# Score products of 64 keys instead of 128: eight small tiles of the array instead of four, in attention and in some steps of a windowed linear attention

## The chip, the cores and the metric

The kernel runs on one core of one Trainium2 chip. The metric is the device time of the whole kernel in microseconds (us), the median of several runs. Smaller is better.

## What is computed

The input is one image of 256 channels and 64 x 64 pixels in float32. Two layers follow one another, and all arithmetic that matters here is float32.

```python
# layer 0: x + L0(group_norm(x)), 8 heads of 32 channels
q, k = sigmoid(Wq x), sigmoid(Wk x);  v = Wv x, normalised per head
for w in (1, 2, 4):                       # windows of 64/w pixels around each pixel
    wk, wkv = box sums of k and of k v^T over the window
    attn = (q . wkv) / (q . wk + 1e-6)
out = Wout concat(attn)
# layer 1 on t = 4096 tokens of 256 channels
dots = einsum('bhid,bhjd->bhij', q, k) * 256 ** -0.5
attn = softmax(dots);  t = t + (attn v) w_out
t = t + mixture of 8 experts, the best 2 per token
```

The change touches two places in which q of some pixels is multiplied with k of others: the windowed sums of layer 0, which the kernel computes as masked scores (q . k for each pixel pair, zeroed outside the window, then times v), and the softmax attention of layer 1.

## The kernel before, in words

The image's 4096 pixels are cut into 8 strips of 8 columns (512 tokens, one "chunk"); each strip has 8 bands of 8 rows, and a strip's part of two such 64-pixel cells is a tile of 128 tokens, 32 in all. Heads have 32 channels, so 4 heads fill the 128 partitions, and both layers go over 2 groups of 4 heads.

**Layer 0** runs from 0 to about 1035 us, one head group after the other. `prepare` makes q, k, v and running sums. `attend` then goes over the three windows. For each it does band steps first (two of the windows: loop over b, scores at line 609, values at line 640), and then strip steps (loop over ix, scores at line 678, values at line 694). A *job* is one tile of 128 keys against a run of query cells of one strip; `packed` puts as many jobs into one *step* as fit into 512 score columns, so a step holds one or two jobs in the strip loop. The step's 4 score banks (one per head, a pool of 6) are masked by `masked` (line 558, on VectorE, or on ScalarE and GpSimd for a head or two), and the values of line 694 are issued one step later, since `behind` puts them into a list that `tick` empties in the middle of the next step. Steps with one job are those of 384 or of 512 query columns: 56 for each head group, 112 in all.

The band steps at line 609 already take 64 keys at a time: for each of 4 heads two products, whose results go to partitions 0 to 63 and 64 to 127 of the head's bank. The strip steps at line 678 take 128 keys at a time.

**Layer 1's attention** runs from 1147 to 2307 us. It is 16 *blocks*: 8 query chunks of 512 by 2 head groups; each block has 32 steps, one for every key tile i. A step is:

```python
for hd in range(4):                          # line 991: 4 products, 128 keys x 512 queries
    sc[hd // 2][:, hd % 2, :] = k[hd, tile i] . q[hd, chunk]
pe[pair] = exp(sc / 16)                      # line 1001, ScalarE, twice 128 x 1024
total[pair] += pe[pair]                      # line 1008, VectorE, twice (not for i = 0 and 31)
# one step later, by tick():
acc[32 hd : 32 hd + 32] += v[i, hd] . pe[hd] # line 959: 4 products, 32 rows of output each
```

The order on TensorE is therefore scores of step i+1, values of step i, scores of i+2, and so on. Scores go to `two_banks` buffers of two banks each; there are 3 of them and a step takes 2. `pe` has 4 buffers, `acc` one. At a block's end come two more groups at line 959 (sums by a matrix of ones), a copy by ScalarE, and, some steps into the next block, a reciprocal (line 1056) and a multiplication (line 1032) on VectorE. In every other block from the fourth on, four steps also carry a projection (`project`, line 940) with an addition and statistics on VectorE.

In both places a product of 32 rows (channels) and 128 columns (keys) uses one row group of the array, and the four heads use its four row groups.

Of the kernel before, what the change touches and what calls it, by code (L numbers as in the profile page):

```python
# [30 lines left out]
P = 128  # L31
# [4 lines left out]
CH = 512  # L36
# [5 lines left out]
CELL = SW * SW  # L42
# [69 lines left out]
def tile_conv_attn_hybrid(ctx: ExitStack, tc: tile.TileContext, a: dict, out: bass.AP):  # L112
    nc = tc.nc
# [26 lines left out]
    def tok(i):  # L140
        return slice(P * i, P * (i + 1))

    def chunk(i):
        return slice(CH * i, CH * (i + 1))
# [18 lines left out]
    def behind(*stages):  # L163

        chains.append(list(stages))
# [20 lines left out]
    with ExitStack() as phase:  # L186
# [23 lines left out]
        with (  # L210
# [23 lines left out]
            for i in range(4):  # L234
                for k in range(KC):
                    at = slice(i * N // 4, (i + 1) * N // 4)
# [45 lines left out]
        rows = big.tile([P, NB, C // D, 4 * IMG], F32, tag="qk", name="rows")  # L282
# [255 lines left out]
        def step_done():  # L538
            tick()
            if chores:  # L540
                chores.pop(0)[1]()
# [3 lines left out]
        def masked(work, scs, used, pieces):  # L545


            turns[0] += 1
            sms = []
            for h, sc in enumerate(scs):  # L550
                sm = work.tile([P, CH], F32, tag="sm", name="sm", bufs=12)
                src, engine = sc, nc.vector
                if h == 1 or h == 3 and turns[0] % 2:
                    nc.scalar.copy(sm[:, :used], sc[:, :used])  # L554
                    src, engine = sm, nc.gpsimd
                for at, n, mk in pieces:
                    to, of = (z[:, at : at + n].rearrange("p (m n) -> p m n", n=mk.shape[-1]) for z in (sm, src))
                    engine.tensor_mul(to, of, mk.unsqueeze(1).to_broadcast(list(to.shape)))  # L558
                sms.append(sm)
            return sms  # L560

        def joined(pieces):

            out = []
            for at, n, mk, key in pieces:
                if out and out[-1][3] == key:
                    out[-1][1] += n
                else:
                    out.append([at, n, mk, key])
            return [piece[:3] for piece in out]  # L570

        def packed(jobs):

            steps = []
            for job in jobs:
                if not steps or sum(j[0] for j in steps[-1]) + job[0] > CH:
                    steps.append([])
                steps[-1].append(job)
            return steps

        def attend(g, work, ps, qk, v, ssum, rec, woT):
            bank = lambda: ps.tile([P, CH], F32, tag="acc", name="ps_acc", bufs=2)
            score = lambda: ps.tile([P, CH], F32, tag="sc", name="ps_sc", bufs=6)
            qT, kT = qk[:, 0], qk[:, 1]
            hs = [slice(D * h, D * (h + 1)) for h in range(4)]
            qcells = qT.rearrange("p (i n) -> p i n", n=CH)
            raw = big.tile([P, NCH, CH], F32, tag="raw", name="raw")
            for w in (2, 1, 0):
# [4 lines left out]
                for b in (1, 2, 0, 3) if r > 1 else ():  # L593
# [8 lines left out]
                    for step in steps:  # L602
                        scs = [score() for _ in range(4)]
                        at, places = 0, []
                        for n, i, lo, hi, kind in step:
                            for h in range(4):
                                for u in range(2):
# [5 lines left out]
                                        start=True,  # L613
                                        stop=True,
                                        skip_group_check=True,
# [44 lines left out]
                for ix in range(NCH):  # L660
                    acc = bank()
                    jobs = []
                    for jx, kind in ((ix - r, 1), (ix, 0), (ix + r, 2)):
                        if 0 <= jx < NCH and (kind or r == 1):
                            for m in (0, 3, 1, 2):
                                c0, c1 = max(0, 2 * m - r), min(SW, 2 * m + 2 + r)
                                key = kind, c0 - 2 * m + r, c1 - 2 * m + r
                                mk = mask[:, kind - 1, _MCELL0[w] :] if kind else mask0
                                mk = mk[:, key[1] : key[2]].rearrange("p n c -> p (n c)")
                                jobs.append((CELL * (c1 - c0), NB * jx + m, c0, c1, mk, key))  # L670
                    begun = [False]
                    steps = packed(jobs)
                    for step in steps:
                        scs = [score() for _ in range(4)]
                        at, places = 0, []
                        for n, i, c0, c1, *mk in step:
                            for h in range(4):
                                nc.tensor.matmul(  # L678
                                    scs[h][:, at : at + n],
                                    kT[hs[h], tok(i)],  # L680
                                    qT[hs[h], CH * ix + CELL * c0 : CH * ix + CELL * c1],
                                    start=True,
                                    stop=True,
                                    skip_group_check=True,
                                )
                            places.append((at, n, i, c0, c1, *mk))
                            at += n
                        sms = masked(work, scs, at, joined((p[0], p[1], *p[-2:]) for p in places))
                        step_done()

                        def use(places=places, sms=sms, acc=acc, begun=begun, ix=ix, last=step is steps[-1], raw=raw, r=r):
                            for at, n, i, c0, c1, *_ in places:
                                for h in range(4):
                                    nc.tensor.matmul(  # L694
                                        acc[hs[h], CELL * c0 : CELL * c1],
                                        v[:, i, hs[h]],
                                        sms[h][:, at : at + n],
                                        start=not begun[0],
                                        stop=last and at == places[-1][0],
                                        skip_group_check=True,  # L700
                                    )
                                begun[0] = True
                            if last and r > 1:
                                nc.vector.tensor_add(raw[:, ix, :], acc, raw[:, ix, :])
                            elif last:
                                nc.scalar.copy(raw[:, ix, :], acc)

                        behind(lambda: None, use)
# [35 lines left out]
        for g in range(KC):  # L744
            with tc.tile_pool(name="c_prep", bufs=1) as prep, psum("c_ps1", 2) as ps:
                of = prepare(g, prep, ps)
            with tc.tile_pool(name="c_work", bufs=1) as work, psum("c_ps2", 1) as ps:
                attend(g, work, ps, *of)
# [33 lines left out]
    with ExitStack() as phase:  # L782
# [9 lines left out]
        qk = big.tile([P, 2, KC, N], F32, name="qk")  # L792
# [5 lines left out]
        with (  # L798
# [23 lines left out]
            for n, by in enumerate((lambda k: ones[:, :1], lambda k: bqk[:, 4 + k : 5 + k])):  # L822
                for k in range(KC):
# [4 lines left out]
                        start=k == 0,  # L828
                        stop=k == KC - 1,
# [11 lines left out]
            for k in range(KC):  # L841
                for j in range(KC):
# [4 lines left out]
                        start=j == 0,  # L847
                        stop=j == KC - 1,
# [11 lines left out]
            for c in range(NCH):  # L860
# [29 lines left out]
                for i in range(NB * c, NB * (c + 1)):  # L890
                    pv = ps.tile([P, CH], F32, tag="mm", name="ps_mm")
                    for k in range(KC):
# [4 lines left out]
                            start=k == 0,  # L897
                            stop=k == KC - 1,
# [47 lines left out]
        with tc.If(tame > 0) as branch:  # L946
            with (
# [5 lines left out]
                def two_banks():  # L953
                    return ps.tile([P, 2, CH], F32, tag="two", name="ps_two", bufs=3)
# [26 lines left out]
                for qc in range(NCH):  # L981
                    for g in range(KC):
# [4 lines left out]
                        for i in range(NT):  # L987
                            sc = [two_banks() for _ in range(2)]
                            for hd in range(4):
                                hs = slice(D * hd, D * (hd + 1))  # L990
                                nc.tensor.matmul(  # L991
                                    sc[hd // 2][:, hd % 2, :],
                                    qk[hs, 1, g, tok(i)],
                                    qk[hs, 0, g, chunk(qc)],
                                    start=True,
                                    stop=True,
                                )
                            pe = work.tile([P, 4, CH], F32, name="pe", bufs=4)
                            pairs = [slice(0, 2), slice(2, 4)]
                            for pair, s in zip(pairs, sc):  # L1000
# [84 lines left out]
        with branch.Else():  # L1085


            with (
# [8 lines left out]
                for hd in range(2 * 4):  # L1097
                    g, hs = hd // 4, slice(D * (hd % 4), D * (hd % 4 + 1))
                    nc.vector.tensor_copy(ka[:D, :], qk[hs, 1, g, :])
                    for qc in range(NCH):  # L1100
                        qa = bigb.tile([D + 1, CH], F32, name="qa")
                        nc.vector.tensor_copy(qa[:D, :], qk[hs, 0, g, chunk(qc)])
                        for i in range(CH // P):
                            for c in range(NCH):
                                sc = ps.tile([P, CH], F32, tag="sc", name="ps_sc")
# [11 lines left out]
                        for i in range(NT):  # L1117
                            sc = ps.tile([P, CH], F32, tag="sc", name="ps_sc")
# [3 lines left out]
                            for j, lhsT in enumerate((v[:, i, D * hd : D * (hd + 1)], ones)):  # L1122
# [4 lines left out]
                                    start=i == 0,  # L1127
                                    stop=i == NT - 1,
                                    skip_group_check=True,
# [10 lines left out]
    with ExitStack() as phase:  # L1140
# [14 lines left out]
        def each(name):  # L1155
            return small.tile([P, NT, NE], F32, name=name)
# [33 lines left out]
        with ExitStack() as routing:  # L1190
# [7 lines left out]
            at = 0  # L1198
# [118 lines left out]
            for n in range(2):  # L1317
                at = each(f"at{n}")
# [12 lines left out]
                for i8 in range(0, NT, G):  # L1331
# [7 lines left out]
                    for i in range(G):  # L1339
# [4 lines left out]
                            start=n == 0 and i8 + i == 0,  # L1344
                            stop=n == 1 and i8 + i == NT - 1,
# [98 lines left out]
        with ExitStack() as ending:  # L1444
# [6 lines left out]
            for b in range(NB):  # L1451
                for i4 in range(0, NCH, 4):
# [4 lines left out]
                    for i in range(4):  # L1457
                        at = NB * (i4 + i) + b
# [43 lines left out]
```

## Time and profile before

| what | us |
|---|---|
| median of 3 runs (lowest, highest) | 2935.82 (2933.38, 2937.23) |
| the profiled execution | 2937.02 |
| its span, first to last instruction | 2935.2 |
| TensorE busy in the span | 2794.7 (95%) |
| VectorE busy | 2083.2 (71%) |
| ScalarE busy | 1533.0 (52%) |
| GpSimd busy | 720.3 (25%) |
| scores of attention, line 991 (4096 MATMULs) | 629.1 |
| values of attention, line 959 (4096 MATMULs) | 546.4 |
| strip scores of layer 0, line 678 (2688 MATMULs) | 245.3 |
| band scores of layer 0, line 609, 64 keys at a time (2560 MATMULs) | 104.9 in its forms |

How to read it: PE is TensorE's products, PEld its weight loads (the load of k or v into the array), DVE VectorE, ACT ScalarE, POOL GpSimd. A row gives line, engine, operation, result and operands, then the shape: "32\*128 32x512" is a product of 32 rows and 128 columns of the array with 512 columns of moving data. Each float32 product appears as two MATMULs and two weight loads, here called its two passes. Products that run beside one another overlap in the records, so their busy time is that of the group, and their ends are modelled while their starts are recorded: durations of groups are best taken from start to start. "Idle before" is the time in which the engine had nothing running ahead of an instruction, with what ended it.

### The profile page before, as it was taken

To read this page: it belongs to the slowest core of one execution; us is meant where nothing else is said; L and a number is where in the kernel's file an instruction comes from. 1 tells how busy PE (TensorE), PEld (TensorE's weight loads), DVE (VectorE), ACT (ScalarE), POOL (GpSimd) and SP (SyncE) were. 2 spreads that over 40 slices of the span, in tenths; PEclk is the share of its full clock that TensorE was granted. 3 is DMA by queue.
4 is the path that set the end of the run, shared out by engine and by line. 5 is a ranking of instruction groups with operands and counts; after the bars stand their busy time and mean duration, and the time that the engine had idled before them with its cause. 6 is when DMAs were issued, how large, how long until landed. Compare 5 with 4: busy or idle time off the path is not lost. (4 is left out here: it accounts for less than half of the span.)

```text
span 2935.2 us, 63107 instructions
## 1 busy us (share of the span) xinstructions
PE 2794.7 (95%) x26358; PEld 1352.3 (46%) x26358; DVE 2083.2 (71%) x3005; ACT 1533.0 (52%) x2134; POOL 720.3 (25%) x816
## 2 busy tenths in 40 slices
PE   6899999989999989999999999999999699999996
PEld 5466442735644354222222222222222268888884
DVE  5776768577677877999999999999999821111113
ACT  3242323124233213888888888888888622222222
POOL 1085858119485621000000000000000022222220
PEclk9999999999999999999999999999999879999997
DMA  5000000000000000000000000000000155555555
GB/s 142 6 3 3 2 3 2 7 1 3 4 2 3 1 19 1 5 5 5 5 5 5 5 5 5 5 5 5 5 5 5 53 182 200 191 189 195 192 196 198
DMA packets 97930, 137.35 MB, mean 47 GB/s; under 512 B 18242, under 2 KB 79272, under 8 KB 97636
## 3 DMA queue, kind: packets, MB, share of 16 engines
q1 hardware_dynamic: 82360, 105.31, 10.9%
q0 software_dynamic: 6912, 18.88, 2.2%
q10 hardware_dynamic: 8364, 9.02, 0.9%
q8 instruction: 210, 3.44, 0.5%
q14 instruction: 84, 0.69, 0.1%
HBM read 115.07 MB, written 18.12 MB: 45 GB/s over the span
## 5 line engine op out<-in xcount | busy, mean ns | idle before, releaser
L1001 ACT ACTIVATE pe<-ps_two 128x1024 f32<-128x1024 f32 x1024 | 993.1, 1022 | 150.0 <-PE ps_two L991 145.4
L1008 DVE TENSOR_TENSOR total<-total,pe 128x1024 f32<-128x1024 f32 x928 | 1058.2, 1217 | 0.0
L991 PE MATMUL ps_two<-qk 32*128 32x512 f32 x4096 | 629.1, 639 | 3.6 <-POOLq L946 1.9
L959 PE MATMUL ps_acc<-pe,v 128*32 128x512 f32 x4096 | 546.4, 605 | 0.1
L554 ACT COPY sm<-ps_sc 128x384 f32<-128x384 f32 (+4 forms) x486 | 232.4, 512 | 459.5 <-PE ps_sc L678 276.4
L558 POOL TENSOR_TENSOR sm<-sm,mask 128x192 f32<-128x192 f32 (+3 forms) x460 | 380.2, 861 | 231.6 <-ACT sm L554 231.0
L991 PEld LDWEIGHTS ps_two<-qk 32*128 32x128 f32 x4096 | 204.8, 183 | 418.7 <-PE ps_two L991 222.2
L558 DVE TENSOR_TENSOR sm<-ps_sc,mask 128x384 f32<-128x384 f32 (+3 forms) x708 | 324.2, 518 | 91.7 <-PE ps_sc L678 90.2
L1417 ACT ACTIVATE hid<-ps_hp,cols 128x256 f32<-128x256 f32 x288 | 136.4, 473 | 382.8 <-PE ps_hp L1416 382.0
L1266 POOL MEMSET on<- 128x256 f32 x1 | 0.3, 311 | 1175.1 <-PE ps_den L959 1175.1
L959 PEld LDWEIGHTS ps_acc<-pe,v 128*32 128x32 f32 x4096 | 80.7, 108 | 389.4 <-issue 376.2
L1416 PE MATMUL ps_hp<-xe,w 128*128 128x256 f32 x1152 | 257.0, 381 | 0.0
L1423 PE MATMUL ps_yp<-w,hid 128*128 128x256 f32 x1152 | 254.6, 379 | 0.0
L678 PE MATMUL ps_sc<-qk 32*128 32x192 f32 (+3 forms) x2688 | 245.3, 446 | 5.2 <-DVE sm L558 2.9
L1423 PEld LDWEIGHTS ps_yp<-w,hid 128*128 128x128 f32 x1152 | 216.4, 190 | 28.1
L1416 PEld LDWEIGHTS ps_hp<-xe,w 128*128 128x128 f32 x1152 | 208.5, 190 | 42.1 <-ACT hid L1417 5.0
L694 PE MATMUL ps_acc<-sm,v 128*32 128x192 f32 (+3 forms) x2688 | 216.6, 423 | 0.8 <-POOL sm L558 0.8
L1395 DVE TENSOR_SCALAR xe<-ps_tp,cols 128x256 f32<-128x256 f32 x72 | 35.9, 540 | 248.8 <-PE ps_tp L1391 228.7
L558 POOL TENSOR_TENSOR sm<-sm,ycut 128x384 f32<-128x384 f32 (+4 forms) x150 | 150.7, 1025 | 140.4 <-ACT sm L554 140.2
L678 PEld LDWEIGHTS ps_sc<-qk 32*128 32x128 f32 x2688 | 126.4, 186 | 124.0 <-DVE sm L558 70.4
L1425 DVE TENSOR_TENSOR y<-ps_yp,b 128x256 f32<-128x256 f32 x72 | 30.6, 425 | 208.1 <-PE ps_yp L1423 208.1
L558 DVE TENSOR_TENSOR sm<-ps_sc,ycut 128x512 f32<-128x512 f32 (+4 forms) x250 | 127.7, 562 | 64.8 <-PE ps_sc L609 62.7
(231 smaller groups left out, 2252.5 us busy)
## 6 DMA issues: line engine op xcount, KB each, us to landing
w<-in_L_ffn_W SPq DMA_DIRECT2D x72, 1024.0 KB
b<-in_L_ffn_b SPq DMA_DIRECT2D x36, 128.0 KB
rows<-in_x SPq DMA_DIRECT2D x16, 256.0 KB
zrows<-z SPq DMA_DIRECT2D x4, 1024.0 KB
y<-yrows SPq DMA_DIRECT2D x8, 512.0 KB
y<-yrows ACTq DMA_DIRECT2D x8, 512.0 KB
rec<-recs SPq DMA_DIRECT2D x60, 64.0 KB
x<-in_x ACTq DMA_DIRECT2D x4, 512.0 KB
```

Of the source, the lines that this page charges most:

```text
L554: nc.scalar.copy(sm[:, :used], sc[:, :used])
L558: engine.tensor_mul(to, of, mk.unsqueeze(1).to_broadcast(list(to.shape)))
L678: nc.tensor.matmul(scs[h][:, at : at + n], kT[hs[h], tok(i)], qT[hs[h], CH * ix + CELL * c0 : CH * ix + CELL * c1], start=True, stop=True, ...
L694: nc.tensor.matmul(acc[hs[h], CELL * c0 : CELL * c1], v[:, i, hs[h]], sms[h][:, at : at + n], start=not begun[0], stop=last and at == plac ...
L959: nc.tensor.matmul(to[D * hd : D * (hd + 1), :], lhsT(hd), rhs[:, hd, :], start=start, stop=stop, skip_group_check=True,)
L991: nc.tensor.matmul(sc[hd // 2][:, hd % 2, :], qk[hs, 1, g, tok(i)], qk[hs, 0, g, chunk(qc)], start=True, stop=True,)
L1001: nc.scalar.activation(pe[:, pair, :], s, AF.Exp, scale=C**-0.5)
L1008: add = nc.vector.tensor_add(to, first[:, pair, :] if i == 1 else to, pe[:, pair, :])
L1395: nc.vector.tensor_scalar(xe[:, k, :], tp[:, k, :], cols[:, gain], cols[:, shift], op0=ALU.mult, op1=ALU.add,)
L1416: nc.tensor.matmul(hp, w1[:, k, tok(n)], x_now[:, k, :], start=k == 0, stop=k == KC - 1)
L1417: nc.scalar.activation(hid[:, n, :], hp, AF.Gelu, bias=cols[:, n : n + 1])
L1423: nc.tensor.matmul(yp, hid[:, n, tok(j)], w2[:, n, :], start=n == 0, stop=n == NH - 1)
```

## The change

Where a strip step has one job, and in every attention step, each product of 128 keys becomes two of 64 keys: keys 0 to 63 of the tile give partitions 0 to 63 of the bank, and keys 64 to 127 give partitions 64 to 127. The moving data (512, or 384, query columns) are the same for both halves. A step issues eight products of 32 rows by 64 columns where it issued four of 32 by 128. Strip steps with two jobs keep products of 128 keys. What is computed, the buffers and the work of the other engines are as before.

```diff
@@ strip steps of layer 0
                         for n, i, c0, c1, *mk in step:
+                            rows = CELL if len(step) == 1 else P
                             for h in range(4):
-                                nc.tensor.matmul(
-                                    scs[h][:, at : at + n],
-                                    kT[hs[h], tok(i)],
-                                    qT[hs[h], CH * ix + CELL * c0 : CH * ix + CELL * c1],
-                                    start=True,
-                                    stop=True,
-                                    skip_group_check=True,
-                                )
+                                for u in range(0, P, rows):
+                                    nc.tensor.matmul(
+                                        scs[h][u : u + rows, at : at + n],
+                                        kT[hs[h], P * i + u : P * i + u + rows],
+                                        qT[hs[h], CH * ix + CELL * c0 : CH * ix + CELL * c1],
+                                        start=True,
+                                        stop=True,
+                                        skip_group_check=True,
+                                    )
@@ attention
                             for hd in range(4):
                                 hs = slice(D * hd, D * (hd + 1))
-                                nc.tensor.matmul(
-                                    sc[hd // 2][:, hd % 2, :],
-                                    qk[hs, 1, g, tok(i)],
-                                    qk[hs, 0, g, chunk(qc)],
-                                    start=True,
-                                    stop=True,
-                                )
+                                for u in range(2):
+                                    nc.tensor.matmul(
+                                        sc[hd // 2][CELL * u : CELL * (u + 1), hd % 2, :],
+                                        qk[hs, 1, g, P * i + CELL * u : P * i + CELL * (u + 1)],
+                                        qk[hs, 0, g, chunk(qc)],
+                                        start=True,
+                                        stop=True,
+                                        skip_group_check=True,
+                                    )
```

## The prediction

> **What bounds the kernel now.** I first took busy time by stage. Attention (lines 983 to 1008 and 959) runs from 1147 to 2307 us; the four other stretches hold all single-block steps of line 678. The columns are the stretch, its length, then busy time of PE, PEld, DVE, ACT and POOL with the number of instructions.
>
> ```profile
> 1147.40:2307.00 1159.60, 1157.80 (x8532) 311.98 (x8536) 1122.94 (x1070) 1008.19 (x1054) 0.00 (x0) 1.00 0.02 5
> 1726.50:1797.30 70.80, 70.80 (x530) 18.42 (x528) 68.90 (x63) 63.07 (x66) 0.00 (x0) 1.00 0.02 5
> 303.70:369.00 65.30, 65.30 (x789) 27.45 (x792) 52.64 (x125) 26.12 (x55) 59.20 (x72) 1.00 0.01 2
> 446.00:506.00 60.00, 60.00 (x544) 15.88 (x538) 49.08 (x89) 25.08 (x50) 52.95 (x50) 1.00 0.01 2
> ```
>
> PE is never out of work in any of them. In one attention block (second line: 32 key tiles for one query chunk and one head group, 70.8 us) DVE is free for only 1.9 us and ACT for 7.7. So PE sets the pace, and DVE is close behind. Busy is not the same as fast, so next the order of time of two steps. The first five rows are PE's, the last two ACT's, from the same stretch.
>
> ```profile
> 1700.61 1.31 PE L991 MATMUL ps_two<-qk 32*128 32x512 f32 x8
> 1701.85 1.07 PE L959 MATMUL ps_acc<-pe,v 128*32 128x512 f32 x8
> 1702.85 1.17 PE L991 MATMUL ps_two<-qk 32*128 32x512 f32 x8
> 1703.94 1.06 PE L959 MATMUL ps_acc<-pe,v 128*32 128x512 f32 x8
> 1704.94 0.70 PE L991 MATMUL ps_two<-qk 32*128 32x512 f32 x2
> ...
> 1701.81 1.94 ACT L1001 ACTIVATE pe<-ps_two 128x1024 f32<-128x1024 f32 x2 [0.15 <-PE ps_two L991]
> 1704.02 1.94 ACT L1001 ACTIVATE pe<-ps_two 128x1024 f32<-128x1024 f32 x2 [0.27 <-PE ps_two L991]
> ```
>
> A float32 product is two MATMULs (a group of 4 is x8). Starts of scores to starts of values take 1.24 us, then 1.10 us: every other group is held up. By its single records heads 0 and 1 start at 1700.609, heads 2 and 3 only at 1700.791, when an exponential (ended 1700.739) has given their score banks back (3 buffers, 2 needed a step). The loop over two steps: heads 0 and 1 of step i start, +1.20 their exponential starts, +1.02 it ends, +0.05 heads 2 and 3 of step i+1 start, +1.06 values start, +1.00 the scores of i+2 start: 4.33 us, 2.166 a step. PE alone would need 1.07 + 1.00 = 2.07.
>
> The form after the change exists already, in the band steps of line 609 (8 products of 32 rows by 64 columns). Same number of query columns, both forms:
>
> ```profile
> 956.94 0.93 PE L678 MATMUL ps_sc<-qk 32*128 32x384 f32 x8
> 957.80 1.06 PE L694 MATMUL ps_acc<-sm,v 128*32 128x512 f32 x8
> ...
> 888.07 0.90 PE L609 MATMUL ps_sc<-qk 32*64 32x384 f32 x16
> 888.90 0.98 PE L640 MATMUL ps_acc<-sm,v 64*32 64x448 f32 x16
> ...
> L678 PEld LDWEIGHTS ps_sc<-qk x2688: 181/184/333, 142.6 to 1005.5; 32*128 32x128 f32 x192
> ...
> L609 PEld LDWEIGHTS ps_sc<-qk x2560: 127/131/132, 232.3 to 946.9; 32*64 32x64 f32 x197
> ```
>
> Start to next group's start: 0.86 us with 128 keys a product, 0.83 with 64 (by the records 857 and 830 ns). A weight load is 181 against 127 ns.
>
> **What the Trainium skill says.** "TensorEngine Tiling (Array Packing)", Available Configurations and Key Properties: 32-row tiles come as four of 128 columns or eight of 64, the tiles work independently, and a change of mode drains the array. The trace agrees and prices the drain: from the last MATMUL's start, less the columns at 1.2 a ns, to the next group's start it is 90 to 96 ns in the 993 changes between lines 991 and 959, and 90 to 97 around line 609; there is a drain before and after. "TensorE: Matmul & The Clock Gate", LDWEIGHTS (loading the stationary operand): a load takes its columns over 1.2 ns, whatever the rows: 107 for 128, 53 for 64. The difference in the trace is 54. The same page, Part 3, gives about 4 ns from tile to tile; the records here show 6.7.
>
> **The change, part by part.** *One score group, nothing waiting.* By the records at 384 columns: first pass to second pass 427 ns before (107 load + 384/1.2), 373 in the 64-key form (53 + 320). The second pass of the last product starts 3 x 6.7 = 20 ns after the first one's before, 7 x 6.7 = 47 after. From there to the next group 410 in both. Sum: -54 + 27 = -27, which is 857 to 830. At 512 columns: 107 + 427 + 20 + 427 + 90 = 1071 (shortest measured group: 1070), after it 53 + 427 + 47 + 427 + 90 = 1044. Line 609 has no group of 512, but 256, 320, 384 and 448 columns give 617, 724, 830 and 937, a straight line that reaches 1044 there. I take -26.5.
>
> *Attention steps in the rhythm above.* Two links of the loop contain a load. Exponential after scores: -54 on the load, and the second pass of heads 0 and 1 ends with the 4th product instead of the 2nd, +13: -40. Heads 2 and 3 to values: -54, and the last product starts 3 x 6.7 after their first instead of 6.7, +13: -40. So -80 per two steps, -40 a step: 2.166 becomes 2.126. PE alone would then need 2.04, so the loop still holds.
>
> *How many steps.* The 510 score groups with a record take 1158 ns on average, 1070 unheld: 510 x 0.088 = 45 us of holding up. Two steps in rhythm hold up 1242 + 1098 - 2 x 1071 = 198 ns, so 45/0.198 x 2 = some 450 steps are in rhythm and 62 (block ends, steps with a projection of line 940) are not. 450 x 40 = 18.0 us, 62 x 26.5 = 1.6 us: **-19.6 us**.
>
> *Is DVE in the way?* Its additions start every 1.135 us, so 2.27 a step in 30 of 32 steps. It falls behind and catches up at the block's end. Block 1726.5: 70.8 - 1.3 = 69.5 us against 68.9 of work: 0.6 us stay free. The second test is the probability buffers (4): the exponential of step i+4 needs the addition of step i. The margin falls from 5.1 us at a block's start to 1.3 at its end (records of all blocks: 1.28 to 2.3); PE being 32 x 0.040 = 1.3 earlier there uses it up just so. I cost this at nothing; if the cover is 0.2 us short in each block, 16 x 0.2 = 3 us come back. ACT has 2 x 1.02 of work in a step of 2.126 and covers.
>
> *Single-block steps of layer 0.* The groups at line 678 of 384 (x640) and 512 columns (x256) are 896/8 = 112 steps. PE is busy throughout the stretches above, POOL for 59.2 of 65.3 and 53.0 of 60.0. 112 x 26.5 = **-3.0 us**; where the second pair waits for a bank as in attention, up to 112 x 40 = 4.5. Lower bound zero, if POOL's masks end last.
>
> *Added.* (512 + 112) x 4 = 2496 more products, 4992 MATMULs and as many loads. No wait is added: the built program has the same semaphore waits before heads 0 and 1 and before heads 2 and 3, and the order on DVE, ACT, POOL and SP is unchanged; no DMA is moved. Queued behind PE's wait are, as before, the values of line 959. Supply of instructions: over the 5120 MATMULs of lines 609 and 640, PE idles 1.8 + 1.6 + 1.1 us under "issue", 0.9 ns each; at worst 4992 x 0.9 = 4.4 us. I take zero, since attention issues 24 MATMULs in 2.1 us where line 609's steps issue 32 in 1.7.
>
> *Sum*: 19.6 + 3.0 = 22.6 us. The profiled execution took 2937.0 us, a span of 2935.2 and 1.8 around it: 2914.4. The median of the runs shown is 1.2 below it: 2935.8 - 22.6 = **2913.2**.
>
> **The rivals.**
> *A, the loop keeps its length and only the drain-to-drain time shrinks.* If exponential and bank release don't move, a step gains 26.5: 624 x 26.5 = 16.5 us, 2919. For it: ACT's start is measured to 50 ns only. Against: the 4th product's second pass starts 480 + 20 ns after the group, before it was 533 + 7.
> *B, DVE becomes the bound.* If DVE can use only half of what is free (its restart at each block costs something that isn't visible as long as it is idle there), 16 x 0.65 = 10 us remain, with 3 of layer 0: 2923. For: the margin of 1.3 us is used to the last. Against: 0.6 us a block stay.
> *C, slower: the supply of PE instructions.* The shortest products, line 374 (1024 MATMULs of 32 columns), idle 9.4 us under "issue", 9.2 ns each. At that price 4992 cost 45.9 us, less 22.6: 23 slower, 2959. It decides from 22.6/4992 = 4.5 ns per MATMUL, in lines 991 and 678. Against: 0.9 ns at lines 609 and 640.
> *D, the halves don't run beside one another at 512 columns* (so that the change doesn't do what it says). A pass of 427 ns more per group would be +270 us; the straight line of line 609 up to 448 columns, in the same banks and tiles, speaks against it so clearly that I give it 1 in 100.
>
> **How the numbers follow.** Forecast 2913.2: 0.77, its own range 2908 to 2918 (all steps at -40 and layer 0 at -4.5: 25 us, 2911, with the runs' scatter of 2 us below it; above, 3 us from the buffers or from supply). A: 0.09. B: 0.06. No gain because several of these meet: 0.02. C: 0.05, D: 0.01. A measurement of this kernel tells 0.2%, 5.9 us, from no change; the forecast, A and B lie beyond it. Faster 0.92, same 0.02, slower 0.06. The range 2907.5 to 2921 takes in A and leaves out B, C and D.
>
> **What would show it.** Score groups of 64 keys with loads of 127 ns; first score to first value of 1.04 us unheld and some 1.20 and 1.06 alternating; step pairs of 4.25 us; attention over 1140 us instead of 1160; DVE free for 0.6 us a block. Wrong if DVE waits vanish and ACT begins to wait for line 1008 (B), if PE idles under "issue" at line 996 (C), or if MATMULs of the two column halves start in turn (D).

## The result, and the profile after

| what | before | after |
|---|---|---|
| median of 6 runs each, side by side (lowest, highest), us | 2936.57 (2933.38, 2940.0) | 2928.53 (2925.42, 2931.12) |
| profiled execution; its span, us | 2937.02; 2935.2 | 2925.42; 2923.6 |
| attention, first exponential to the end of the last, us | 1158.8 | 1150.2 |
| four stretches of strip steps with one job, us | 242.9 | 239.7 |
| TensorE MATMULs | 26358 | 31350 |

The ratio is 0.9972, 95% interval 0.9959 to 0.9985: 8.0 us less, where 22.6 were forecast. The sign is right; most of the size is missing.

The profile page of the changed kernel, groups of instructions (busy us, mean ns | idle us before them and what ended it). The additions, the scores and the exponentials now stand at lines 1014, 996 and 1007, the values at 962, the strip scores at 681.

```profile
L1007 ACT ACTIVATE pe<-ps_two 128x1024 f32<-128x1024 f32 x1024 | 992.4, 1021 | 142.4 <-PE ps_two L996 127.5
L1014 DVE TENSOR_TENSOR total<-total,pe 128x1024 f32<-128x1024 f32 x928 | 1058.1, 1217 | 0.0
L996 PE MATMUL ps_two<-qk 32*64 32x512 f32 x8192 | 620.3, 613 | 3.6 <-POOLq L949 1.8
```

The products have the new form (32\*64), 8192 of them, and TensorE's products are idle for only 3.6 us in all ahead of line 996. The same view of time by stretch as before, for attention and for one block of it (length, then busy PE, PEld, DVE, ACT, POOL):

```profile
1146.00:2299.00 1153.00, 1151.07 (x12640) 275.40 (x12628) 1124.55 (x1072) 1008.84 (x1055) 0.00 (x0) 1.00 0.02 5
1431.80:1502.00 70.20, 70.20 (x788) 16.36 (x784) 68.79 (x63) 63.02 (x66) 0.00 (x0) 1.00 0.02 6
```

A block that took 70.8 us takes 70.2; the work of VectorE in it, 68.8 us, has not shrunk. The order of time inside such a block, TensorE's rows first, then ScalarE's:

```profile
1600.43 1.13 PE L996 MATMUL ps_two<-qk 32*64 32x512 f32 x16
1601.49 1.07 PE L962 MATMUL ps_acc<-pe,v 128*32 128x512 f32 x8
1602.49 1.28 PE L996 MATMUL ps_two<-qk 32*64 32x512 f32 x16
1603.71 1.07 PE L962 MATMUL ps_acc<-pe,v 128*32 128x512 f32 x8
1604.70 1.13 PE L996 MATMUL ps_two<-qk 32*64 32x512 f32 x16
...
1601.61 4.00 ACT L1007 ACTIVATE pe<-ps_two 128x1024 f32<-128x1024 f32 x4 [0.27 <-PE ps_two L996]
```

Two steps take 1604.70 - 1600.43 = 4.27 us; the pair shown before took 4.33, and 4.25 was forecast. By single records of the 407 undisturbed pairs in attention, 63 take 4.24 to 4.25 us, as forecast; 169 take about 4.27, 49 about 4.30 and 125 about 4.32. The mean is 4.286, and it was 4.321 before (198 pairs at about 4.305, 185 at about 4.33). One group is held up and one nearly not (1.22 and 1.06 to the values): the old rhythm, slightly shorter.

A correction to the description of the kernel before: a strip has 4 bands of 16 rows, one tile of 128 tokens each; 8 is the number of its cells of 8 by 8 pixels.

### The profile page after: what moved, and what is told of

Read it like the earlier page. It is cut to its first block, busy times and chain, and to the rows that moved or that the text cites. A ratio compares the mean times of both kernels' runs of the same rounds, so it can differ in the third digit from the quotient of the medians.

```text
span 2923.6 us, 73315 instructions
## 1 busy us (share of the span) xinstructions
PE 2781.4 (95%) x31350; PEld 1306.2 (45%) x31350; DVE 2082.9 (71%) x3005; ACT 1531.7 (52%) x2134; POOL 720.5 (25%) x816
## 4 chain that ended last, share of the span: by engine, by line
PE 58%; DMA 1%; DVE 1%; ACT 1%; issue 0%; POOL 0%; DVEq 0%; SPq 0%; ACTq 0%; POOLq 0%
PE ps_two L996 20%; PE ps_acc L962 17%; PE ps_yp L1429 9%; PE ps_hp L1422 8%; PE ps_den L943 1%; PE ps_den L962 1%; PE ps_acc L1346 1%; DMA y<-yrows 1%; ACT z L1230 1%; PE ps_tp L1397 1%; DVE t L1466 0%; DMA xs<-zrows,source 0%; PE ps_two L943 0%; DMA yrows<-y,target 0%; DVE rec L1043 0%
## 5 line engine op out<-in xcount | busy, mean ns | idle before, releaser
L996 PE MATMUL ps_two<-qk 32*64 32x512 f32 x8192 | 620.3, 613 | 3.6 <-POOLq L949 1.8
L996 PEld LDWEIGHTS ps_two<-qk 32*64 32x64 f32 x8192 | 166.8, 130 | 420.7 <-PE ps_two L996 378.7
L681 PE MATMUL ps_sc<-qk 32*64 32x384 f32 (+3 forms) x3584 | 240.8, 461 | 4.6 <-DVE sm L558 2.9
L681 PEld LDWEIGHTS ps_sc<-qk 32*64 32x64 f32 (+1 forms) x3584 | 116.7, 159 | 122.5 <-DVE sm L558 69.7
```

The costliest lines, as they stand in the source:

```text
L681: nc.tensor.matmul(scs[h][u : u + rows, at : at + n], kT[hs[h], P * i + u : P * i + u + rows], qT[hs[h], CH * ix + CELL * c0 : CH * ix + C ...
L996: nc.tensor.matmul(sc[hd // 2][CELL * u : CELL * (u + 1), hd % 2, :], qk[hs, 1, g, P * i + CELL * u : P * i + CELL * (u + 1)], qk[hs, 0, g ...
```

## The experiments

All ratios are against the kernel before, run beside; the bracket behind a ratio is its 95% interval. Three theories were tested first, numbered 1 to 3 in this order in the texts below: that something lengthens the link from scores to exponential (**increments**: TensorE signals each product whose count anyone waits for, and each signal costs time); that each of several products running beside one another ends later than the one before by more than it started later (**ends**); and that VectorE stands in the way at a block's beginning (**totals**).

**1. No fallback branch, changed kernel and kernel before.** The program ends attention with a branch that is not entered with these inputs: it recomputes attention with a running maximum. Its instructions wait on the same count of TensorE's products as attention does. Both kernels leave that branch out, so their output covers only inputs that do not need it.

```diff
-        with tc.If(tame > 0) as branch:
+        with tc.If(tame > 0):
...
-        with branch.Else():
-            ...
```

> The changed kernel without the branch for untamed scores (a fallback that this data never enters; it is left out). With it go the waits of that branch, which share the numbering of TensorE's semaphore with attention and force extra increments there: heads 0 and 1 then count up once instead of 2.45 times on average. Theory 1 (each extra increment holds the exponential back by 26 ns): the exponential starts 1154 ns after its score group in every regular step, a pair of steps takes 4.24 us instead of 4.27 to 4.32, attention is some 8.5 us shorter than in the changed kernel: 2920 us. Theory 2 (the eight products finish later by themselves, whatever counts): the start stays at 1180 to 1232 ns, 2928 us. Theory 3 (VectorE has become the bound): the exponential starts earlier but ScalarE begins to wait for line 1008's additions, 2928 us.

> The kernel before without the same never-entered branch (left out). Heads 0 and 1 count up once instead of 1.49 times. Theory 1: exponential at 1174 ns after its group in every regular step (now 1174 or 1200), 0.49 x 26 / 2 x 450 steps = 3 us shorter: 2933.5. Theories 2 and 3: 2936.5, no change. With the run beside it, theory 1 gives the change itself 13 to 14 us of gain when nothing extra is counted, where 8 were measured.

Measured: 2921.3 us for the changed kernel (ratio 0.9943, 0.993 to 0.9956) and 2932.5 for the one before (0.9979, 0.9972 to 0.9985), with 2937.92 beside them. The order of time of the changed kernel without the branch:

```profile
1601.56 1.23 PE L996 MATMUL ps_two<-qk 32*64 32x512 f32 x16
1602.72 1.06 PE L962 MATMUL ps_acc<-pe,v 128*32 128x512 f32 x8
1603.72 1.16 PE L996 MATMUL ps_two<-qk 32*64 32x512 f32 x16
1604.81 1.07 PE L962 MATMUL ps_acc<-pe,v 128*32 128x512 f32 x8
```

The pair from 1601.56 to its repeat is 1604.81 + 1.00 - 1601.56 = 4.25 us; by single records 383 of 407 pairs take 4.244 to 4.250 (before, without the branch, most take 4.304 to 4.306). The start of the exponential after its scores, sorted by how often the products of heads 0 and 1 signal:

```
signals of heads 0, 1        1      2      3      4
before   (2 products)     1174   1200      -      -   ns; 263, 249 groups
after    (4 products)     1154   1180   1206   1232   ns; 100, 207, 80, 125 groups
after, no branch          1154 in 479 of 512 groups
```

Each further signal costs 26 ns; without the branch, one signal of these products is left in every group. The mean is 1.49 signals before (1187 ns) and 2.45 after (1192 ns): more of the new products have to signal for the branch's waits. "TensorE: Matmul & The Clock Gate", Part 3, The cost: per-tile semaphore tail, states 26.3 ns for each increment and that they serialize; the trace agrees. The prediction used another figure of the same Part 3, the launches from tile to tile, and not this term.

The whole came out where theory 1 put it, at 2920, but not for its reason alone: attention became 3.1 us shorter than in the changed kernel (1147.1 against 1150.2), where the theory had 8.5. Where the rest lies isn't shown: the profiled executions of these two kernels have spans of 2923.0 and 2923.6 us.

**2. The same branch, moved away from attention's count.** The kernel can compute everything again; the fallback stands under a second condition after attention.

```diff
-        with branch.Else():
+        with tc.If(tame < 1):
```

> The changed kernel with everything computed, but the fallback in a second branch of its own after attention instead of an else. Its waits then have numbers of their own. Theory 1: the same attention as without the fallback, plus a second branch not taken, 1 to 5 us: 2921 to 2925. Theories 2 and 3: 2929 to 2933.

Measured: 2929.11 us, 0.9972 (0.9962 to 0.9982), no better than the changed kernel as a whole, although attention from block 2 on takes 1009.7 us, just as without the branch (1011.7 in the changed kernel, 1019.0 before). So the link is freed, but 2.0 us come of it in attention, and these are lost behind it. There the next stage waits for the second condition, and its first instruction starts 16.7 us after the last exponential, not 1.2 as in the changed kernel:

```profile
2314.38 0.31 POOL L1272 MEMSET on<- 128x256 f32 x1 [1180.24 <-DVEq L1091]
```

Line 1091 is that condition. From the last exponential to the first product of the experts it takes 68.3 us here, 65.0 in the changed kernel and 63.7 without the branch.

What stops attention is seen in the waits of VectorE in attention without the branch (us in all, times, longest):

```profile
DVE total L1014 <- PE ps_den L962: 16.9, 14, 1.2
DVE total L1014 <- ACT pe L1007: 7.3, 2, 5.8
```

In the changed kernel the same view is

```profile
DVE total L1014 <- ACT pe L1007: 26.0, 15, 6.1
DVE total L1014 <- PE ps_den L962: 1.2, 1, 1.2
```

In 14 of the block beginnings VectorE waits 1.2 us, not for the first exponential, but until TensorE has read the last block's `total` at line 962 to sum it: there is one buffer of it. VectorE's 68.8 us of work and this 1.2 make 70.0, and that is what a block takes without the branch:

```profile
1579.40:1649.40 70.00, 70.00 (x788) 15.70 (x784) 68.79 (x63) 63.07 (x66) 0.00 (x0) 1.00 0.02 6
```

**3. A second place for `total`**, in a half of another buffer that is free then, for head group 1 except in chunk 4; once without the fallback branch and once with everything computed.

```diff
-                        total = work.tile([P, 4, CH], F32, name="total")
+                        if g and qc != 4:
+                            half = slice(4 * CH, 8 * CH) if qc < 4 else slice(0, 4 * CH)
+                            total = act[:, 0, half].rearrange("p (h c) -> p h c", c=CH)
+                        else:
+                            total = work.tile([P, 4, CH], F32, name="total")
```

> The changed kernel without the never-entered fallback (left out), and with a second place for the sums of a block: blocks of the second head group keep their total in the unused half of act, except at query chunk 4, so blocks 8, 9 and 10 of 0 to 15 share one buffer as before. Theory A (without the extra increments VectorE's sums have become the bound, because a block's first addition waits until TensorE has read the last block's total out of the one buffer: 68.8 us of work + 1.21 of waiting = 70.03 a block): VectorE's idle time falls below 1.21 us in the blocks with a second place, an even block takes 69.7 us instead of 70.03, and blocks 9 and 10 stay at 1.21. In all some 4 us less: 2917 beside a kernel before of 2938. Theory B (1.21 us is only what the score loop leaves): nothing changes.

> Everything computed: the fallback in a branch of its own, and the second place for the sums. Theory A: 4 us less than with the branch alone, 2925 beside a kernel before of 2938. Theory B: 2929. Either is the fastest kernel that computes everything only if it stays clear of the changed kernel's 8 us of gain.

Measured: 2920.09 us (0.9943, 0.9929 to 0.9956) and 2923.57 (0.9961, 0.9947 to 0.9975), with 2936.55 beside them; attention from block 2 on 1006.7 in both. VectorE's waits without the branch, and one block:

```profile
DVE total L1018 <- ACT pe L1011: 12.3, 13, 5.8
DVE act L1018 <- ACT pe L1011: 6.6, 8, 1.0
DVE total L1018 <- PE ps_den L962: 2.4, 2, 1.2
```

```profile
1576.50:1646.30 69.80, 69.80 (x788) 15.72 (x784) 68.91 (x63) 63.11 (x66) 0.00 (x0) 1.00 0.02 6
```

The wait for line 962 is down from 16.9 to 2.4 us. Blocks take 69.78 and, with a projection, 73.96 us (70.03 and 74.20 with one place); the two blocks for which chunk 4's place is shared stay at 70.02 and 74.20, a control inside the same run. That the single place is a bound is shown. Removing it is worth 0.25 us a block, 3.0 us in attention by the traces where 4 were expected, and VectorE is still idle for only 0.89. The whole times don't tell it: the ratio without the branch is 0.9943 with one place and with two. The version with everything computed has the lowest median of the complete kernels here, 13.0 us under the kernel before, but its interval overlaps that of the changed kernel.

**4. Sixteen products of 32 keys**, without the branch, to tell the ends apart from the signals.

```diff
-                                for u in range(2):
+                                for u in range(4):
...
-                                        sc[hd // 2][CELL * u : CELL * (u + 1), hd % 2, :],
-                                        qk[hs, 1, g, P * i + CELL * u : P * i + CELL * (u + 1)],
+                                        sc[hd // 2][D * u : D * (u + 1), hd % 2, :],
+                                        qk[hs, 1, g, P * i + D * u : P * i + D * (u + 1)],
```

> The changed kernel without the never-entered fallback (left out), attention with 32 keys a product: sixteen products of 32 rows by 32 columns. By the sum of the prediction a score group with nothing to wait for takes 27 + 427 + 15 x 6.7 + 427 + 90 = 1071 ns, back where 128 keys were. The exponential's start tells what the missing 20 ns of its link are. Theory C (each product more ends 17 ns after the one before, not 6.7): 1174 - 16.7 - 533 + 453 + 7 x 16.7 = 1194 ns. Theory D (halving a product's columns costs a fixed 20 ns behind its launch): 453 + 47 + 674 = 1174. A pair of steps 4.28 (C) or 4.26 us (D) instead of 4.24; 2923 to 2926 beside a kernel before of 2938, where 64 keys gave 2921.

Measured: 2924.43 us, 0.9961 (0.9947 to 0.9974). The order of time:

```profile
1599.91 1.28 PE L996 MATMUL ps_two<-qk 32*32 32x512 f32 x32
1601.12 1.06 PE L962 MATMUL ps_acc<-pe,v 128*32 128x512 f32 x8
1602.11 1.16 PE L996 MATMUL ps_two<-qk 32*32 32x512 f32 x32
1603.20 1.07 PE L962 MATMUL ps_acc<-pe,v 128*32 128x512 f32 x8
1604.20 1.28 PE L996 MATMUL ps_two<-qk 32*32 32x512 f32 x32
```

A pair is 4.29 us, and the exponential starts 1194 ns after its scores in nearly every group. One sum covers all three forms: with one signal, it starts 624 ns after the first launch of a second pass (533, 480 or 454 ns after the group's start) and 16.7 ns later for each product of heads 0 and 1 beyond the first (533 + 624 + 17 = 1174 with 2 products; 480 + 624 + 50 = 1154 with 4; 454 + 624 + 117 = 1195 with 8). The two constants come from the forms with 2 and 4 products; the 1194 of 8 products was expected from them (theory C). Launches are 6.7 ns apart; ends, as the consumer sees them, 17. Had the ends been spaced like the launches, 8 products would have given 1174 (theory D), so that theory falls.

**5. The two parts alone.** In the first, layer 0's strip products stay at 128 keys (`rows = P`); in the second, attention's do.

> Only attention in eight products; the single-block steps of layer 0 as before. All theories: attention keeps its gain of about 8.6 us and its extra increments. By the prediction's sum layer 0 gives 3.0 us back: 2931.5; by the traces (attention starts 1.7 us earlier in the changed kernel) it is nearer 2930.2.

> Only the single-block steps of layer 0 in eight products, attention as before. By the stretches of the traces 3.2 us less than before in every trace: 2934.7 beside a kernel before of 2938; attention 1159 us. If what layer 0 gains is taken back before attention starts, 2938.

Measured: attention alone 2929.89 us (0.9975, 0.9966 to 0.9984); layer 0 alone 2935.36 (0.9998, 0.999 to 1.0007). Attention alone gives what both give. Yet layer 0's four stretches are 3.2 us shorter (239.65 against 242.90) with the change. They are lost in the band section that follows between two strips of head group 0: from its first line 609 to the next strip 75.57 us before and with attention alone, 78.14 with layer 0 alone, 78.47 in the changed kernel. TensorE's rows there in the kernel before, then with layer 0 alone:

```profile
421.12 1.99 PE L628 MATMUL ps_acc<-qk,ssum 32*32 32x64 f32 x128
423.04 0.66 PE L640 MATMUL ps_acc<-sm,v 64*32 64x256 f32 x16
423.63 1.01 PE L609 MATMUL ps_sc<-qk 32*64 32x448 f32 x16
```

```profile
420.08 0.66 PE L640 MATMUL ps_acc<-sm,v 64*32 64x256 f32 x15
421.43 0.40 PE L640 MATMUL ps_acc<-sm,v 64*32 64x256 f32 x1 [0.69 <-issue]
421.76 1.01 PE L609 MATMUL ps_sc<-qk 32*64 32x448 f32 x16
```

After a burst of 128 short MATMULs at line 628 the last of 16 at line 640 comes late, with nothing but "issue" ahead of it (a stall, below). From line 640's first to line 609 it is 423.63 - 423.04 = 0.59 us before and 421.76 - 420.08 = 1.68 here. It happens again 15 us later: twice 1.1 us, and 0.4 at the burst before, make the 2.6. In the changed kernel the three bursts lose 0.7, 1.1 and 1.1 us, which is the whole of 78.47 - 75.57. All seven traces of kernels with this layer 0 lose at the same three bursts (78.1 to 79.2 us); the four in which head group 0 is as before do not (75.57 or 75.58).

**6. Does the number of instructions do it, or the earlier end of the strip?** Three kernels with attention as before: layer 0 changed in head group 1 only; the kernel before with each score product of the one-job steps of head group 0 issued twice (same number of instructions as the change, but a longer strip); and layer 0 changed with the first four such steps issued twice (64 MATMULs and 64 loads, 128 instructions more).

```diff
-                            rows = CELL if len(step) == 1 else P
+                            rows = CELL if len(step) == 1 and g else P
@@ doubled, from the kernel before
+                            twice = 2 if len(step) == 1 and g == 0 else 1
...
+                                for u in [0] * twice:
@@ shifted, from the layer 0 change
-                                for u in range(0, P, rows):
+                                for u in list(range(0, P, rows)) * (2 if more else 1):
```

> Attention as before; single-block strip steps of layer 0 with 64 keys a product in head group 1 only. Disputed: why the band section between the two strips of head group 0 takes 78.1 us with layer 0 changed and 75.6 before. Theory S (supply: what counts is how many instructions TensorE has been given ahead of the section): group 0 keeps its 75.6 us, its strips 63.7 and 57.7; group 1's strips 63.2 and 56.7; group 1's own band section may now grow by up to 2.5. Theory T (the strips end earlier, so that the section's first products come before something they share with other engines): group 0 the same 75.6, and group 1's section grows as group 0's did, to some 78. Both need 75.6 in group 0; anything near 78 there would refute both and put the loss on the rest of the program.

> The kernel before, but in head group 0 each score product of a single-block strip step is issued twice, with 128 keys and the same result, so that TensorE gets exactly the number of instructions of the changed kernel there, while the strips become longer by some 15 to 30 us instead of shorter. Theory S (number of instructions ahead of the section): the band section of head group 0 takes about 78.1 us, with idle time of some 1.1 us under issue at line 640 after bursts of line 628. Theory T (earlier end of the strip): 75.6 us, without that idle time.

> Attention as before, layer 0 changed, and the first four single-block steps of head group 0 issue their eight products twice: 32 products, 128 more TensorE instructions ahead of the band section, some 4 us more in the first strip. Theory S: the section's idle time depends on where its bursts of short products fall in the stream, so it moves: some other length than 78.1, by 0.5 us or more, between 75.6 and 80, with the idle time at other bursts. Theory T: the strip ends about 3.4 us later than before, so the section is back at 75.6. If it stays at 78.1 with idle time at the same bursts, both fall.

Measured, one run each beside 2940.0: 2934.31, 2978.53 and 2938.8 us. Head group 0's band section takes 75.57, 78.92 and 75.59 us. Waits of TensorE's loads in it, doubled and then shifted:

```profile
PEld ps_acc L640 <- issue: 17.8, 29, 1.7
PEld ps_acc L641 <- issue: 14.2, 26, 0.7
```

The doubled kernel's strip is 15.4 us longer (84.38 against 68.96) and the stall is there, so an earlier end is not its cause. With as many instructions ahead of the section as the change has, it stalls; with 128 more, it doesn't. The shifted kernel alone would not decide: its 75.59 is the figure that the earlier end (theory T) named, and the idle time at other bursts that theory S looked for didn't appear in this section. In the first of the three, head group 1's section stayed at 75.75 with 192 more MATMULs, and as many loads, ahead of it, so more instructions are not in themselves a loss.

Why that place stalls was not tried by a run of its own, but the kept traces point to how instructions arrive. The profile page counts the packets that bring them (packets, MB, share); queue 8 in the kernel before, and with attention alone:

```profile
q8 instruction: 210, 3.44, 0.5%
q8 instruction: 242, 3.96, 0.6%
```

The 8192 MATMULs and loads that attention adds cost 32 packets, and the 1792 of layer 0 alone cost 7 (217): 256 of TensorE's instructions each. A burst at line 628 with its loads is 256 instructions too. Ahead of the section, the change and the doubled kernel add 384 instructions, one and a half packets, and stall; the shifted kernel adds 512, two whole packets, and doesn't. And in all eight traces with the stall the lost time at each of the three bursts ends 1.2 to 1.6 us after such a packet has landed (once 1.8). So the position of the bursts against the packets' borders is the likely cause. It isn't proven, since no run moved the packets alone; and why head group 1's section is spared isn't known.

## Why the prediction was wrong in size

*Right.* The score group that nothing holds up: forecast 1044 ns, measured 1043 to 1045 in most. The load: 127 to 133 ns, median 130, at line 996. "Heads 2 and 3 to values: ... -40": 1058 became 1017 to 1018. The drain between groups, 89 to 97 ns. Layer 0's steps themselves: -3.0 forecast, -3.2 measured.

*Failed: "Exponential after scores: ... -40".* It became 1192 from 1187 on average, +5. This step failed first, and two terms were missing from it. The load's 54 are there; the prediction added 13 for two further launches, but the end that ScalarE sees moves by 2 x 16.7 = 33, so that -20 is the most (1174 to 1154, shown by the two kernels without the branch; the 16.7 is confirmed by 32 keys). And 2.45 signals a group instead of 1.49 take another 25. The prediction had made sure that no wait is *added*; it hadn't counted which products *signal*. A pair of steps therefore gains not 80 but 40 - 5 = 35 ns on average, as measured: 4321 to 4286. With the prediction's own counts, 450 steps at 17.5 and 62 at 26.5 ns give 9.5 us instead of 19.6; attention became 8.5 shorter.

*Failed: "I cost this at nothing" for VectorE.* The 0.6 us that it called free is not usable: a block's first addition waits for line 962 to read the one `total`. As long as that place is the only one, a block takes 70.0 us (74.2 with a projection) even with the link mended, against 70.75 (74.8) before. Eight of each, 8 x 0.72 + 8 x 0.6, allow some 10.6 us; -19.6 was out of reach. That is rival B, which names a restart at each block as the cost, and which I held for 6 in 100; that its 10 us come within half a microsecond of the bound is in part luck, since it guessed that half of the idle time is usable. In the changed kernel itself it is not yet what binds (line 962 ends one wait only); it becomes so as soon as the first link is mended, which is why mending it alone brought only 2.0 us.

*Failed: supply, "I take zero".* True for attention, where TensorE's products showed no idle time under "issue" at line 996. Not for line 640, which the change doesn't touch: 2.6 to 2.9 us there take back layer 0's 3.2. The prediction priced supply at lines 609, 640 and 374; the bursts of line 628, ahead of which the kernel before already idles 5.1 us under "issue", were not among them.

*The sum.* Attention 8.5 less, layer 0 3.2 less and 2.9 more (78.47 - 75.57): 8.8, beside 8.0 by the medians. The profiled executions lie 11.6 apart; the rest is spread over stages that the change doesn't touch, where kernels of this study scatter: the first strip steps start between 139.6 and 142.6 us. Rival A is half right: the exponential's link didn't move, the other one did; its 26.5 ns a step became 17.5, as the loop still goes through the exponential, and layer 0's 3.0 us were lost again. D is refuted by the group of 1044 ns. Of C, a loss by supply happened, at another place and at a sixteenth of its 45.9 us.

*Open.* With its own place for `total` a block still takes 69.78 us where 70.75 - 1.25 = 69.5 would follow from the forecast; what holds the last 0.3 wasn't tried. Leaving the fallback branch out also shortens the whole by 8 us against the version that has it under a second condition (2921.3 and 2929.11; 3.5 us in the pair with a second place for `total`), at equal attention. By the traces 4.6 us of it (7.0 in the other pair, 69.8 against 62.8) lie between the last exponential and the experts, where the second condition stands; the traced executions are not those of the medians, so the rest stays open.

## What to carry to other kernels

When one product becomes two, price the last end as its consumer sees it (launch, pass, and a term for each product beside it), and count the products that signal in the built program, including those made to signal by waits in code that never runs. Before calling a few tenths of an engine's idle time free, find out what ends that idle time: if it is a buffer with a single place, the idle time is a bound, and the engine is already as good as full. And compare the unchanged sections too, since added instructions can cost time at a later burst of short ones.

## What the runs showed of the hardware

Each further signal by TensorE delayed the consumer of a group by 26 ns (1154, 1180, 1206 and 1232 ns for 1 to 4). Products launched 6.7 ns apart kept their reader waiting 16.7 ns more for each. Of 128, 64 and 32 keys a product, 64 was best here: groups that nothing held up took 1070, 1044 and 1070 to 1089 ns. TensorE's instructions came in packets of 256 (8192 more, 32 packets more), and 2.6 to 2.9 us of lost time came and went with the number of instructions ahead of an unchanged section.
